# PSUM split by the engine that writes it, and a graph layer's blocks staggered over three blocks' time

## The chip, the cores and the metric

The kernel runs on one core of a Trainium2 chip. The metric is the device time of one execution in microseconds, from the first to the last instruction of the program with what lies directly around it. Three runs of the kernel before gave 17895.24, 17900.07 and 17902.10 us; their median, 17900.07 us, is the time it is measured against. One further execution was recorded by the hardware profiler and took 17875.51 us; every row quoted below comes from that one.

## What is computed

One layer of a graph network on 50,000 nodes of 128 features and 1,650,000 edges, sorted by destination. The reference, cut:

```python
Xs = X[src]
m_data = Xs @ W_data.T + b_data
m_ctrl = Xs @ W_control.T + b_control
msg = jnp.where((edge_types == 0)[:, None], m_data, m_ctrl)
agg = jax.ops.segment_sum(msg, dst, num_segments=X.shape[0])
out = jax.nn.relu(agg + (X @ W_self.T + b_self))
return _layernorm(X + out)
```

The kernel sums rows of X first, for each destination and edge type apart, and multiplies the sums by the weights afterwards.

## The kernel before, in words

The edges are cut into 448 blocks. A block covers at most 124 destination nodes and has two steps of 14 columns of 128 edges, so 28 columns; what is left over of its edges (63 per step with the late ones, "fillers") is put into free places of the columns by arithmetic. All work of a block is spread over four engines.

- **POOL** (GpSimd) does nothing in the loop but fetch rows: one indirect DMA per column (`gathers`, L499) brings 128 rows of X into a slot `y`. Seven columns make a pass and share a slot; a block has four passes (q = 0 to 3), and there are ten slots (`SLOTS`). The first DMA of a pass waits until PE has finished with the slot's pass of ten passes ago; the other six wait for nothing.
- **PE** (TensorE) multiplies each column by its one-hot matrix (`products`, L518: in fp32, which makes two weight loads and two matmuls a column, 28 instructions a pass), adds the counts (L522), spreads the filler list over the partitions (`spread`, L353), counts replaced places (`left_out_columns`, L390), builds the correction for them (`left_out_numbers`, L406 and L409) and computes the finished block (`own_part` and `layer`, L543 to L554).
- **DVE** (VectorE) makes the one-hot matrices two blocks ahead (`onehot` L474, `counts` L482), places the fillers up to five blocks ahead (`fill`, L362 to L383), turns L390's result into a matrix (`left_out_matrix`, L397 and L398), moves the node features (`positions`, L468), adds the products to the running sums (`begin_sums` L538, `add` L527), and does ReLU, moments and normalisation (`moments`, L559 to L567, `store`, L589).
- **ACT** takes one square root per pair of blocks (L580), **SP** issues the plain loads and stores.

Every ten blocks `columns` (L240 to L341) prepares a group of blocks, with a matrix `rank` on PE (L287, L289).

The order on each engine is written out by hand in the main loop of `straight` (from `for b in range(NBLK)`), and each engine runs its instructions strictly in that order. Semaphores are placed from the tiles: an instruction that writes a PSUM tile waits for the earlier readers of that tile's bank. In the kernel before one bank, `small`, holds four things: constants that DVE reads in `onehot` and `fill` (`num_ps`, `rank_no_ps`), a small copy that DVE writes in `fill` (L362), the filler list that PE writes in `spread`, and the column that PE writes in L390 and DVE reads in L397. So PE's L390 stands behind DVE's `oh`, and PE's L353 behind DVE's `at`.

In block b the kernel before adds the last products of block b-1 to the sums first, computes the layer of b-1 on PE after the second pass, and adds the first step of block b as soon as its second pass is done.

Of the kernel before, what the change touches and what calls it, by code (L numbers as in the profile page):

```python
# [11 lines left out]
F32 = mybir.dt.float32  # L12
BF16 = mybir.dt.bfloat16
# [19 lines left out]
R = 14  # L33
# [59 lines left out]
def straight(ctx, tc, c, x, x_t, edges_t, edges_f, dst_first, first_p, out):  # L93
# [22 lines left out]
    ps_r = ctx.enter_context(tc.tile_pool(name="ps_r", bufs=1, space=bass.MemoryType.PSUM))  # L116
# [12 lines left out]
    FILL = Q * FX + C1  # L129
# [36 lines left out]
    nc.vector.tensor_scalar(row_of[:, 1, :], c["ident"][:GB, :GB], float(COLS), None, op0=ALU.mult)  # L166

    loads = {}
    col_g, rk_g, stay_g, cb_g, vp_g, late_g = {}, {}, {}, {}, {}, {}
    stats = keep.tile([P, 2, 2, GROUPS], F32, name="stats")  # L170
    nc.vector.memset(stats, 0.0)
# [83 lines left out]
    def packed(src, col):  # L255
# [5 lines left out]
        nc.vector.scalar_tensor_tensor(v, src, float(COLS), lim, op0=ALU.mult, op1=ALU.add)  # L261
        return v

    def columns(g):

        a = loads.pop(g)
# [7 lines left out]
        def first_of_f(rel, d):  # L274
# [3 lines left out]

        h = eds.tile([P, GB, Q, H], BF16, name="h_loop", bufs=1)
        nc.vector.memset(h, 0.0)
        nc.vector.tensor_tensor(h[:, :, :, :R], a["s"].rearrange(steps, r=R1)[:, :, :, :R],
                                a["d"].rearrange(steps, r=R1)[:, :, :, :R], op=ALU.is_equal)
        rank = ps_r.tile([P, GB * Q, H], F32, name="rank")
        hs_ = h.rearrange("p b q r -> p (b q) r")
        nc.tensor.matmul(rank, below, hs_, start=True, stop=False)  # L287
        for r in range(R):
            nc.tensor.matmul(rank[:, :, r + 1:], ones_b, hs_[:, :, r:r + 1].to_broadcast([P, GB * Q, R - r]),  # L289
                             start=False, stop=r == R - 1)  # L290
# [55 lines left out]
    def spread(b):  # L346

        if plain(b):
            return
        g, i = divmod(b, GB)  # L350
        vf = lists[b % 2][:, :Q * FX]
        for m in range(3):
            nc.tensor.matmul(vf, row_of[:, min(m, 1), i:i + 1].to_broadcast([GB, P]), vp_g[g][:, m, :], start=m == 0, stop=m == 2)  # L353

    def fill(b):

        if plain(b):
            return
        g, i = divmod(b, GB)
        two = lists[b % 2]  # L360
        vf, cb = two[:, :Q * FX], two[:, Q * FX:]
# [9 lines left out]
        nc.vector.tensor_reduce(v, new, AX.X, ALU.add)  # L371
        vi = fil.tile([P, C1], I32, name="vi")
        nc.vector.tensor_tensor(vi, v, stay_g[g][:, i, :], op=ALU.add)
        idx = fil.tile([P, C1], I32, name="idx", bufs=RAHEAD + 2)
        nc.vector.tensor_single_scalar(idx, vi, COLS.bit_length() - 1, op=ALU.logical_shift_right)
        nc.vector.scalar_tensor_tensor(col_g[g][:, i, :], idx, -float(COLS), vi, op0=ALU.mult, op1=ALU.add)
        idxs[b] = idx

        old = fil.tile([P, C1, FX], F32, name="old", bufs=1)
        nc.vector.tensor_tensor(old, m, cb[:, :, None].to_broadcast([P, C1, FX]), op=ALU.mult)  # L380
        by = fil.tile([P, Q, FX], BF16, name="by")
        with nc.allow_low_precision(reason="whole numbers below 256, one of them not 0"):
            nc.vector.tensor_reduce(by, old.rearrange("p (q r) f -> p q f r", r=R1), AX.X, ALU.add)  # L383
        bys[b] = by
# [60 lines left out]
    def window(b):  # L445
        if b % SPAN:
            return
        n = min(SPAN, NBLK - b)
        w = b // SPAN
        _, regs = nc.values_load_multi_w_load_instructions(  # L450
            base_i[0:1, w, :1 + n], engines=[SP], min_val=0, max_val=(N - B) * ROW,
            skip_runtime_bounds_check_because=CLAMPED)
        for i in range(n):
            bases[b + i] = regs[1 + i]
        at = nc.s_assert_within(regs[0], 0, (N - WIDE) * 4, skip_runtime_bounds_check_because=CLAMPED)
        xw = stp.tile([P, WIDE], F32, name="xw")
        nc.sync.dma_start(xw.bitcast(U8), x_t_bytes[:, bass.ds(at, 4 * WIDE)])
        wides[w] = xw

# [114 lines left out]
    def pair(b):  # L574

        return together(b) if b == together(b)[-1] else ()
# [19 lines left out]
    def find_bad():  # L596
# [29 lines left out]
        nc.vector.tensor_reduce(total, gap, AX.X, ALU.add)  # L626
        nc.vector.tensor_copy(c["bad"], total)

    columns(0)
    spread(1)  # L630
    fill(1)
# [1 line left out]
    window(0)  # L633
    onehot(0)
    counts(0)
    left_out_columns(1)
    left_out_matrix(1)
    positions(0)
    clear_sums()
    spread(2)  # L640
    fill(2)
    for b in range(1, AHEAD):
        onehot(b)
        counts(b)
    made, fresh = 2, [2]
    ready = []
    for b in range(NBLK):
        if b == NBLK - 2:
            find_bad()
        if b == NBLK - 1:  # L650
            if pair(b - 2):
                store(pair(b - 2))
                ready.extend(pair(b - 2))
            while ready:
                store_rows(ready.pop(0))
        if b + 3 < NBLK:
            window(b + 3)
        g, i = divmod(b, GB)
# [4 lines left out]
        for f in fresh:  # L663
            spread(f)
        if b > 0:
            add(b - 1, steps_of(b - 1)[-1])
        begin_sums(b)
        if b == NBLK - 1:
            layer(b - 1)
            moments(b - 1)  # L670
            root(pair(b - 1))
            own_part(b)
            store(pair(b - 1))
            for done in pair(b - 1):
                store_rows(done)
            for step, ks in passes_of(b):
                if ks:
                    products(b, step, ks)
                    if step not in steps_of(b)[-1:] and ks[-1] == chunks_of(b, step)[-1]:
                        add(b, step)  # L680
            break
        if b + AHEAD < NBLK:
            onehot(b + AHEAD)
            counts(b + AHEAD)
        last = steps_of(b)[-1:]
        for q, (step, ks) in enumerate(passes_of(b)):
            if ks:
                products(b, step, ks)
            if q == 0:
                for f in due:  # L690
                    left_out_columns(f)
                for f in fresh:
                    fill(f)
            if q == 1 and b > 0:
                layer(b - 1)
            if q == 1:
                left_out_numbers(b + 1)
            if ks and step not in last and ks[-1] == chunks_of(b, step)[-1]:
                add(b, step)
            if q == 1 and b > 0:  # L700
                moments(b - 1)
            if q == 1:
                for f in due:
                    left_out_matrix(f)
            if q == 1 and b + 1 < NBLK:
                positions(b + 1)
                left_out_rows(b + 1)
            if q == 2 and i == GB // 2 - 1 and g + 1 < GROUPS:
                columns(g + 1)
            if q == 1 and b > 1 and pair(b - 2):  # L710
                store(pair(b - 2))
                ready.extend(pair(b - 2))
            if q == 3 and b > 0 and pair(b - 1):
                root(pair(b - 1))
            if q == 3 and ready:
                store_rows(ready.pop(0))
    b = NBLK - 1
    add(b, steps_of(b)[-1])
    layer(b)
    moments(b)  # L720
    root(pair(b))
# [332 lines left out]
```

## Time and profile before

| | |
|---|---|
| median of three runs | 17900.07 us |
| the profiled execution | 17875.51 us |
| its span, first to last instruction | 17873.8 us |
| share of the span busy: PE / weight loads / DVE / POOL | 39% / 34% / 66% / 66% |
| mean granted TensorE clock | 0.598 |
| indirect DMAs on POOL | 12,516 and 6 for the last block |
| mean time per block (28 columns) | 17873.8 / 447.1 = 39.98 us |

No engine is busy for more than two thirds of the span, and the busy shares are the same in all forty slices of it, so that one block looks much like any other. A row of the timeline gives the start, the duration, the engine, the line and operation, and, in brackets, how long the engine had been idle before and what ended that; "issue" is idle time for which the profile shows no semaphore, "remote" a semaphore whose sender it could not tell. PEld is the weight load, which shares PE's instruction stream. In the table of windows, (x) after a busy time is the number of instructions in that stretch.

### The profile page before, as it was taken

To read this page: it belongs to the slowest core of one execution; us is meant where nothing else is said; L and a number is where in the kernel's file an instruction comes from. 1 tells how busy PE (TensorE), PEld (TensorE's weight loads), DVE (VectorE), ACT (ScalarE), POOL (GpSimd) and SP (SyncE) were. 2 spreads that over 40 slices of the span, in tenths; PEclk is the share of its full clock that TensorE was granted. 3 is DMA by queue.
4 is the path that set the end of the run, shared out by engine and by line. 5 is a ranking of instruction groups with operands and counts; after the bars stand their busy time and mean duration, and the time that the engine had idled before them with its cause. 6 is when DMAs were issued, how large, how long until landed. Compare 5 with 4: busy or idle time off the path is not lost.

```text
span 17873.8 us, 103324 instructions
## 1 busy us (share of the span) xinstructions
PE 6946.3 (39%) x34670; PEld 6006.5 (34%) x34671; DVE 11876.6 (66%) x12324; ACT 69.8 (0%) x231; POOL 11880.6 (66%) x12532
## 2 busy tenths in 40 slices
PE   3433434333343333333333333343333333333334
PEld 2333333333333333333333333333333333333333
DVE  7666666666666666666666666666666666666665
ACT  0000000000000000000000000000000000000000
POOL 6666666666666666666666666666666666666666
PEclk6656555555565555666555555565555555555556
DMA  2211112112121111212212112121121211212111
GB/s 53 52 50 50 51 50 52 50 50 52 50 51 50 50 51 50 52 50 52 51 50 52 50 50 52 50 52 50 50 51 50 52 50 50 52 50 51 50 50 47
DMA packets 474808, 905.71 MB, mean 51 GB/s; under 512 B 204473, under 2 KB 260872, under 8 KB 474270
## 3 DMA queue, kind: packets, MB, share of 16 engines
q0 software_dynamic: 400736, 821.40, 18.1%
q1 hardware_dynamic: 73096, 77.42, 1.5%
q8 instruction: 279, 4.57, 0.1%
q14 instruction: 259, 2.12, 0.0%
q10 hardware_dynamic: 438, 0.20, 0.0%
HBM read 869.76 MB, written 28.44 MB: 50 GB/s over the span
## 4 chain that ended last, share of the span: by engine, by line
DVE 51%; another core or an unknown queue 27%; issue 17%; PE 5%; DVEq 0%; DMA 0%; ACT 0%; ACTq 0%
DVE cnt L482 14%; DVE oh L474 9%; DVE m L364 4%; DVE v_new L371 4%; DVE new L367 4%; DVE old L380 4%; PE acc L518 4%; DVE sums L527 2%; DVE sums L538 1%; DVE z L398 1%; DVE st L562 1%; DVE h L560 1%; DVE xT L468 1%; DVE h L559 0%
## 5 line engine op out<-in xcount | busy, mean ns | idle before, releaser
L499 POOL DMA_INDIRECT y<-in_x,idx x12516 | 11873.2, 949 | 5958.3 <-issue 3574.2
L518 PE MATMUL acc<-oh,y 128*128 128x128 f32 x25044 | 5433.2, 373 | 4761.1 <-issue 4725.3
L518 PEld LDWEIGHTS acc<-oh,y 128*128 128x128 f32 x25044 | 4793.6, 277 | 7175.2 <-issue 5937.1
L527 DVE TENSOR_TENSOR sums<-acc,sums 128x192 f32 x895 | 314.8, 352 | 4137.2 <-remote 4003.0
L482 DVE TENSOR_REDUCE cnt<-oh 128x256 bf16<-128x3584 f32 x448 | 2807.1, 6266 | 15.4
L474 DVE TENSOR_TENSOR oh<-col,small 128x3584 f32<-128x3584 f32 x448 | 1737.4, 3878 | 255.4 <-remote 185.4
L383 DVE TENSOR_REDUCE by<-old 128x126 bf16<-128x1764 f32 x446 | 1466.5, 3288 | 15.5
L353 PE MATMUL small<-v_f,row_of 10*128 10x126 bf16 x1338 | 231.4, 287 | 2709.3 <-DVE st L562 1642.5
L353 PEld LDWEIGHTS <-row_of 10*128 10x128 bf16 x1338 | 127.1, 112 | 2895.1 <-issue 2882.5
L364 DVE TENSOR_TENSOR m<-rk,small 128x1764 f32<-128x1764 f32 x446 | 888.5, 1992 | 17.7 <-remote 1.7
L367 DVE TENSOR_TENSOR new<-m,small 128x1764 f32<-128x1764 f32 x446 | 888.1, 1991 | 15.2
L371 DVE TENSOR_REDUCE v_new<-new 128x28 f32<-128x1764 f32 x446 | 887.9, 1991 | 15.2
L380 DVE TENSOR_TENSOR old<-m,small 128x1764 f32<-128x1764 f32 x446 | 884.8, 1984 | 0.0
L390 PE MATMUL small<-ones_b,by 128*126 128x1 bf16 x446 | 72.6, 163 | 1917.8 <-DVE oh L474 1352.2
L522 PE MATMUL acc<-cnt,to_row 128*128 128x64 bf16 x1790 | 293.2, 224 | 669.7 <-issue 665.9
L554 PE MATMUL po<-wmsgT,sums 128*124 128x128 f32 x1792 | 428.5, 367 | 82.5 <-issue 79.7
L522 PEld LDWEIGHTS <-to_row 128*128 128x128 bf16 x1790 | 225.7, 126 | 678.6 <-issue 646.4
L559 DVE COPY h<-po 124x128 f32<-124x128 f32 x448 | 125.8, 281 | 439.0 <-PE acc L518 306.2
L554 PEld LDWEIGHTS po<-wmsgT,sums 128*124 128x124 f32 x1792 | 314.0, 241 | 196.8 <-issue 169.7
L415 DVE TENSOR_TENSOR pl<-pl,xT 128x248 f32<-128x248 f32 x446 | 189.4, 425 | 208.1 <-remote 136.3
L552 PE MATMUL po<-bias,sums 3*124 3x128 f32 x896 | 281.7, 396 | 91.4 <-issue 90.9
L289 PEld LDWEIGHTS <-ones_b 128*128 128x128 bf16 x630 | 82.0, 150 | 639.7 <-issue 620.2
(142 smaller groups left out, 3673.6 us busy)
## 6 DMA issues: line engine op xcount, KB each, us to landing
y<-in_x,idx POOLq DMA_INDIRECT x12516
xw<-in_x_t SPq DMA_DIRECT2D x56, 496.0 KB
out<-o SPq DMA_DIRECT2D x448, 62.0 KB
sdt<-in_edges_t SPq DMA_DIRECT2D x45, 420.0 KB
sdt_f<-in_edges_f SPq DMA_DIRECT2D x45, 14.8 KB
first_i<-in_dst_first SPq DMA_DIRECT2D x1, 450.0 KB
y<-in_x,sdt POOLq DMA_INDIRECT x6
w_all<-in_L_gnn_W_data ACTq DMA_DIRECT2D x1, 64.0 KB
```

What stands on the lines that cost most here:

```text
L364: nc.vector.tensor_tensor(m, rk_g[g][:, i, :, None].to_broadcast([P, C1, FX]), rank_no_ps[:, None, :].to_broadcast([P, C1, FX]), op=ALU.is ...
L367: nc.vector.tensor_tensor(new.rearrange("p (q r) f -> p q r f", r=R1), m.rearrange("p (q r) f -> p q r f", r=R1), vf.rearrange("p (q f) -> ...
L371: nc.vector.tensor_reduce(v, new, AX.X, ALU.add)
L380: nc.vector.tensor_tensor(old, m, cb[:, :, None].to_broadcast([P, C1, FX]), op=ALU.mult)
L383: nc.vector.tensor_reduce(by, old.rearrange("p (q r) f -> p q f r", r=R1), AX.X, ALU.add)
L474: nc.vector.tensor_tensor(oh, col_g[g][:, i, :, None].to_broadcast([P, C1, 2 * W]), num_ps[:, None, :].to_broadcast([P, C1, 2 * W]), op=AL ...
L482: nc.vector.tensor_reduce(cnt, ohs[b].rearrange("p (q r) w -> p q w r", r=R1), AX.X, ALU.add)
L499: copy = nc.gpsimd.indirect_dma_start(out=y[:r, k % PASS, :].bitcast(U8), out_offset=None, in_=x_rows, in_offset=bass.IndirectOffsetOnAxis ...
L518: nc.tensor.matmul(acc[:, :2, :].rearrange("p t w -> p (t w)"), y[:r, k % PASS, :], ohs[b][:r, column(k), :], start=k == of_step[0], stop= ...
L522: nc.tensor.matmul(acc[:, 2, :], to_row[:, t, :], cnts[b][:, q, t * W:(t + 1) * W], start=t == 0, stop=t == 1)
L527: nc.vector.tensor_tensor(part, accs.pop((b, q)), part, op=ALU.add)
L554: nc.tensor.matmul(po, a[:, t, :B], c["wmsgT"][:, t * D:(t + 1) * D], start=False, stop=t == 1)
```

## The change

Three things are changed together; no instruction of arithmetic is added or removed.

First, the PSUM bank `small` becomes two: `fixed`, which only DVE writes (the constants and the copy of L362, two of them by turns), and `made`, which only PE writes (one filler list in place of two, the matrix `rank`, which had a bank of its own, and the column of `left_out_columns`).

Second, the work of a block is spread over more blocks. DVE adds both steps of block b-1 in block b, after its fills, in one go with `begin_sums`; PE computes the layer of block b-2 in block b; the correction of b-1 is multiplied out in block b (before, that of b+1). `left_out_matrix` runs one block after its `left_out_columns`. `onehot` and `counts` come first in DVE's block, then `fill`.

Third, buffers follow: one more one-hot matrix (`ohp`), four `by`, two wide feature tiles in place of three. The first half of `columns` becomes `loops` and `ranks`, one block earlier.

```diff
-    ohp = ctx.enter_context(tc.tile_pool(name="ohp", bufs=AHEAD + 1))
+    ohp = ctx.enter_context(tc.tile_pool(name="ohp", bufs=AHEAD + 2))
...
-    small = keep_ps.tile([P, 2 * W + FX + 2 * FILL + 2], F32, name="small")
-    num_ps, rank_no_ps = small[:, :2 * W], small[:, 2 * W:2 * W + FX]
-    lists = [small[:, 2 * W + FX + i * FILL:][:, :FILL] for i in range(2)]
-    sums_at = [small[:Q * FX, 2 * W + FX + 2 * FILL + i:][:, :1] for i in range(2)]
+    fixed = keep_ps.tile([P, 2 * W + FX + 2 * C1], F32, name="fixed")
+    num_ps, rank_no_ps = fixed[:, :2 * W], fixed[:, 2 * W:2 * W + FX]
+    olds = [fixed[:, 2 * W + FX + i * C1:][:, :C1] for i in range(2)]
+    made_ps = keep_ps.tile([P, Q * FX + GS * (R + 1) + 2], F32, name="made")
...
-        by = fil.tile([P, Q, FX], BF16, name="by")
+        by = fil.tile([P, Q, FX], BF16, name="by", bufs=4)
...
-        xw = stp.tile([P, WIDE], F32, name="xw")
+        xw = stp.tile([P, WIDE], F32, name="xw", bufs=2)
...
-        if b > 0:
-            add(b - 1, steps_of(b - 1)[-1])
-        begin_sums(b)
...
+        for f in fresh:
+            spread(f)
+            fill(f)
         for q, (step, ks) in enumerate(passes_of(b)):
             if ks:
                 products(b, step, ks)
-            if q == 0:
...
-            if q == 1 and b > 0:
-                layer(b - 1)
-            if q == 1:
-                left_out_numbers(b + 1)
-            if ks and step not in last and ks[-1] == chunks_of(b, step)[-1]:
-                add(b, step)
...
+            if q == 1 and b > 0:
+                if b > 1:
+                    layer(b - 2)
+                left_out_numbers(b - 1)
+            if q == 2:
+                for f in late_pcs:
+                    left_out_matrix(f)
                 for f in due:
                     left_out_columns(f)
...
+            if q == 2 and b > 0:
+                positions(b - 1)
+                left_out_rows(b - 1)
+                begin_sums(b - 1)
+                for step in steps_of(b - 1):
+                    add(b - 1, step)
+                if b > 1:
+                    moments(b - 2)
```

How the instructions stand, first on PE around the filler list and the column of replaced places; `small` and `made` are the PSUM banks, `acc` the products' bank, and the names in brackets are what the instruction waits for (`landed` the rows' arrival). Before, from the end of one block into the next:

```order
L353 MATMUL small<-v_f,row_of 128x126 [waits DVE_49]
L518 MATMUL acc<-oh,y 128x128 [waits landed0,PE_sequencer_49]
...
L390 LDWEIGHTS by
L390 MATMUL small<-ones_b,by 126x1 [waits DVE_49]
L518 MATMUL acc<-oh,y 128x128 [waits landed1,PE_sequencer_49]
...
L554 MATMUL po<-wmsgT,sums_187 124x128 x2
```

The change, the same stretch:

```order
L361 MATMUL made<-v_f,row_of 128x126
L525 MATMUL acc<-oh,y 128x128 [waits landed2,PE_sequencer_49,DVE_49]
...
L525 MATMUL acc<-oh,y 128x128 [waits landed3,PE_sequencer_49]
...
L561 MATMUL po<-wmsgT,sums_185 124x128 x2
...
L525 MATMUL acc<-oh,y 128x128 [waits landed4,PE_sequencer_49]
...
L397 LDWEIGHTS by
L397 MATMUL made<-ones_b,by 126x1 [waits DVE_49]
L525 MATMUL acc<-oh,y 128x128 [waits landed5,PE_sequencer_49]
```

The column's matmul has moved from behind the first pass to behind the third, and waits there for DVE's copy `at` of the same block (L404) instead of its `oh`. The list's matmul waits for DVE no more, since that wait already stood ahead of it. The first product of a block, which did not wait for DVE, now has a third wait, for the sums that free its bank `acc`; the third wait takes an instruction of its own on PE, 398 more in the whole program, and DVE has 445 more of that kind.

On DVE, from the sums into the next block; `acc` are the products, `pl` the correction, `po` the layer's output. Before:

```order
L527 TENSOR_TENSOR sums_188<-acc,sums_188 128x3x64 [waits PE_49]
...
L538 TENSOR_TENSOR sums_189<-pl,sums_188 128x3x124 [waits DVE_49]
L474 TENSOR_TENSOR oh<-col,small 128x3584 [waits PE_49]
L482 TENSOR_REDUCE cnt<-oh 128x256 [waits DVE_49]
L362 COPY small<-cb 128x28 [waits PE_49]
...
L527 TENSOR_TENSOR sums_189<-acc,sums_189 128x3x64 [waits PE_49]
L559 COPY h<-po 124x128 [waits PE_49]
...
L415 TENSOR_TENSOR pl<-pl,xT 128x2x124 [waits DVE_49,PE_49]
```

The change:

```order
L422 TENSOR_TENSOR pl<-pl,xT 128x2x124 [waits DVE_49,PE_49]
...
L545 TENSOR_TENSOR sums_186<-pl,sums_185 128x3x124 [waits DVE_49]
...
L534 TENSOR_TENSOR sums_186<-acc,sums_186 128x3x64 [waits DVE_49]
...
L534 TENSOR_TENSOR sums_186<-acc,sums_186 128x3x64 [waits DVE_49]
L566 COPY h<-po 124x128
...
L481 TENSOR_TENSOR oh<-col,fixed 128x3584
L489 TENSOR_REDUCE cnt<-oh 128x256 [waits DVE_49]
L369 COPY fixed<-cb 128x28
...
L374 TENSOR_TENSOR new<-m,made 128x1764 [waits DVE_49,PE_49]
```

Of six places in a block at which DVE waits for PE two are left: the correction (L422) and the filler list (L374). The order of POOL's instructions and what they wait for is as before.

More of the change, by code (lines that the diff above doesn't have):

```diff
@@ L168, in straight @@
     loads = {}
+    hs_g = {}
     col_g, rk_g, stay_g, cb_g, vp_g, late_g = {}, {}, {}, {}, {}, {}
@@ L262, in packed, with loops, ranks @@
         return v
+    def loops(g):
+        a = loads[g]
+        steps = "p b (q r) -> p b q r"
+        h = eds.tile([P, GB, Q, H], BF16, name="h_loop", bufs=1)
+        nc.vector.memset(h, 0.0)
+        nc.vector.tensor_tensor(h[:, :, :, :R], a["s"].rearrange(steps, r=R1)[:, :, :, :R],
+                                a["d"].rearrange(steps, r=R1)[:, :, :, :R], op=ALU.is_equal)
+        hs_g[g] = h.rearrange("p b q r -> p (b q) r")
+    def ranks(g):
+        hs_ = hs_g[g]
+        nc.tensor.matmul(rank, below, hs_, start=True, stop=False)
+        for r in range(R):
+            nc.tensor.matmul(rank[:, :, r + 1:], ones_b, hs_[:, :, r:r + 1].to_broadcast([P, GB * Q, R - r]),
+                             start=False, stop=r == R - 1)
     def columns(g):
@@ L277, in first_of_f @@
                    begin_p.rearrange("b (q g) -> b q g", q=Q)[:, :, g:g + 1].to_broadcast([GB, Q, FX]))
[L281 to L290, printed above, removed]
+        hs_ = hs_g.pop(g)
         col, rel, nz = columns_of(a["d"], a["t"], first_of, "")
@@ L350, in spread @@
         g, i = divmod(b, GB)
-        vf = lists[b % 2][:, :Q * FX]
         for m in range(3):
-            nc.tensor.matmul(vf, row_of[:, min(m, 1), i:i + 1].to_broadcast([GB, P]), vp_g[g][:, m, :], start=m == 0, stop=m == 2)
+            nc.tensor.matmul(vf_ps, row_of[:, min(m, 1), i:i + 1].to_broadcast([GB, P]), vp_g[g][:, m, :], start=m == 0, stop=m == 2)
     def fill(b):
@@ L359, in fill @@
         g, i = divmod(b, GB)
-        two = lists[b % 2]
-        vf, cb = two[:, :Q * FX], two[:, Q * FX:]
+        vf, cb = vf_ps, olds[b % 2]
         nc.vector.tensor_copy(cb, cb_g[g][:, i, :])
@@ L627, in find_bad @@
         nc.vector.tensor_copy(c["bad"], total)
+    loops(0)
+    ranks(0)
     columns(0)
@@ L644, in straight @@
         counts(b)
-    made, fresh = 2, [2]
-    ready = []
-    for b in range(NBLK):
+    made, fresh = 2, [1, 2]
+    late_pcs, ready = [], []
+    for b in range(NBLK - 1):
         if b == NBLK - 2:
             find_bad()
[L650 to L655, printed above, removed]
         if b + 3 < NBLK:
@@ L684, in straight @@
             counts(b + AHEAD)
-        last = steps_of(b)[-1:]
+        if i == GB // 2 - 2 and g + 1 < GROUPS:
+            loops(g + 1)
+        for f in fresh:
+            spread(f)
+            fill(f)
         for q, (step, ks) in enumerate(passes_of(b)):
@@ L688, in straight @@
                 products(b, step, ks)
-            if q == 0:
+            if q == 1 and b > 0:
[5 more added lines that the diff above has]
+                    left_out_matrix(f)
                 for f in due:
                     left_out_columns(f)
-                for f in fresh:
-                    fill(f)
-            if q == 1 and b > 0:
-                layer(b - 1)
-            if q == 1:
-                left_out_numbers(b + 1)
-            if ks and step not in last and ks[-1] == chunks_of(b, step)[-1]:
[L699 to L714, printed above, removed]
+                late_pcs = due
+                if i == GB // 2 - 2 and g + 1 < GROUPS:
+                    ranks(g + 1)
+            if q == 2 and b > 0:
[6 more added lines that the diff above has]
+                    moments(b - 2)
+                if b > 2 and pair(b - 3):
+                    store(pair(b - 3))
+                    ready.extend(pair(b - 3))
+                if b > 1 and pair(b - 2):
+                    root(pair(b - 2))
+                if i == GB // 2 - 1 and g + 1 < GROUPS:
+                    columns(g + 1)
             if q == 3 and ready:
@@ L717, in straight @@
     b = NBLK - 1
-    add(b, steps_of(b)[-1])
+    layer(b - 2)
+    left_out_numbers(b - 1)
+    positions(b - 1)
+    left_out_rows(b - 1)
+    begin_sums(b - 1)
+    for step in steps_of(b - 1):
+        add(b - 1, step)
+    moments(b - 2)
+    if pair(b - 3):
+        store(pair(b - 3))
+        ready.extend(pair(b - 3))
+    if pair(b - 2):
+        root(pair(b - 2))
+    layer(b - 1)
+    if pair(b - 2):
+        store(pair(b - 2))
+        ready.extend(pair(b - 2))
+    while ready:
+        store_rows(ready.pop(0))
+    positions(b)
+    begin_sums(b)
+    moments(b - 1)
+    root(pair(b - 1))
+    own_part(b)
+    store(pair(b - 1))
+    for done in pair(b - 1):
+        store_rows(done)
+    for step, ks in passes_of(b):
+        if ks:
+            products(b, step, ks)
+            if ks[-1] == chunks_of(b, step)[-1]:
+                add(b, step)
     layer(b)
```

21 lines of the change are left out of this document (2 added, 19 removed).

## Prediction

> **What bounds the kernel now.** I read the page's busy sums and chain first, then the costliest groups, then the waits of POOL's fetches, a stretch of the timeline around one stop, and last a table of windows.
>
> ```profile
> span 17873.8 us, 103324 instructions
> PE 6946.3 (39%) x34670; PEld 6006.5 (34%) x34671; DVE 11876.6 (66%) x12324; ACT 69.8 (0%) x231; POOL 11880.6 (66%) x12532
> DVE 51%; another core or an unknown queue 27%; issue 17%; PE 5%; DVEq 0%; DMA 0%; ACT 0%; ACTq 0%
> ```
>
> No engine is full, and the chain puts half of the span on DVE. That reading I don't take: DVE's 11,876.6 us are 26.6 us in each of the 447 blocks of the main loop, and a block takes 17,873.8 / 447.1 = 39.98 us, so the chain runs through DVE only because its work happens to end late. What has no slack is POOL:
>
> ```profile
> L499 POOL DMA_INDIRECT y<-in_x,idx x12516: 939/947/1582, 3.3 to 17832.7; - x199
> its engine sat idle before it (us, times) until:
>   issue: 3575.7, 11728
>   remote: 1937.7, 403
>   PE acc L522: 200.2, 102
>   PE small L353: 96.9, 20
> ```
>
> A fetch lasts 0.947 us, and between two lie 3575.7 / 11,728 = 0.305 us for which nothing is shown: one fetch every 1.252 us, whatever the rest does. 12,516 of them are 15,670 us. From the first to the last pass 17,829 us, so that some 2,160 us are stops. Nearly all of it is waits of 1,937.7 / 403 = 4.8 us, about one a block: 28 x 1.252 = 35.05 us of fetches and one stop of 4.83 us above the usual gap give 39.9 us, which is the block. So the question is what makes POOL stop once a block.
>
> ```profile
> 9013.04 0.95 POOL L499 DMA_INDIRECT y<-in_x,idx  x1 [0.30 <-issue]
> 9013.93 0.29 PEld L518 LDWEIGHTS acc<-oh,y 128*128 128x128 f32 x1 [2.51 <-issue]
> 9014.64 0.37 PE L518 MATMUL acc<-oh,y 128*128 128x128 f32 x1 [1.73 <-issue]
> 9016.03 0.29 PEld L518 LDWEIGHTS acc<-oh,y 128*128 128x128 f32 x1 [1.81 <-issue]
> 9018.83 1.65 PE L518 MATMUL acc<-oh,y 128*128 128x128 f32 x7 [0.33 <-issue]
> 9019.07 0.36 DVE L527 TENSOR_TENSOR sums<-acc,sums 128x192 f32 x1 [13.27 <-remote]
> 9019.12 0.95 POOL L499 DMA_INDIRECT y<-in_x,idx  x1 [5.13 <-remote]
> 9019.92 3.88 DVE L474 TENSOR_TENSOR oh<-col,small 128x3584 f32<-128x3584 f32 x1
> 9023.85 0.16 PE L390 MATMUL small<-ones_b,by 128*126 128x1 bf16 x1 [3.37 <-DVE oh L474]
> ```
>
> This is one stop. Up to 9018.8 PE creeps: each load or matmul takes 0.7 us or more beyond itself, with no wait named ("issue"). POOL issues its last fetch of the stretch at 9013.04, then stands 5.13 us. At 9018.83, 4.8 us after that fetch ended, everything lets go at once: PE runs seven matmuls on end, DVE gets an answer that it had stood 13.27 us for, POOL starts again. The same picture returns once a block. How much PE gets done between two such stops the windows show (columns: PE, PEld, DVE, ACT, POOL busy with their instructions, clock, DMA share, GB/s):
>
> ```profile
> 9218.40:9231.80 13.40, 10.02 (x63) 9.39 (x64) 13.05 (x6) 0.00 (x0) 10.05 (x11) 0.67 0.20 49
> 9231.80:9258.30 26.50, 4.05 (x15) 2.40 (x14) 12.77 (x20) 0.00 (x0) 16.44 (x18) 0.55 0.25 67
> 9417.80:9448.60 30.80, 15.23 (x72) 13.64 (x73) 29.13 (x34) 0.29 (x1) 23.15 (x25) 0.56 0.20 50
> 9448.60:9457.70 9.10, 1.52 (x7) 1.32 (x6) 1.88 (x8) 0.00 (x0) 4.07 (x4) 0.69 0.14 36
> 9016.00:9018.80 2.80, 0.74 (x2) 0.86 (x3) 0.00 (x0) 0.00 (x0) 0.00 (x0) 0.50 0.00 0
> 9018.80:9021.20 2.40, 1.65 (x7) 1.46 (x7) 2.10 (x3) 0.00 (x0) 1.78 (x2) 0.50 0.11 27
> ```
>
> Two blocks, each a fast stretch and a creep. In the first PE ran 63 + 64 = 127 instructions at 9.5 a us, then 29 in 26.5 us, 1.1 a us. In the second, where it was held by waits in between, 145 in 30.8 us, then 13 in 9.1 us. So the fast stretch ends neither after a time nor after a fixed count: 18 instructions more go with 17.4 us more, about one a us, the pace of the creep. I read it as a store that a stop fills: 127 - 13.4 x 1.03 = **113 instructions**, and one a us trickles in. DVE ran 6 instructions in the one stretch and 34 in the other, which shows no charge for them. In the emptiest part of the stop, 9016.0 to 9018.8, the DMA engines moved nothing. What the store is I can't see; that its price is 4.83 / 113 = 0.043 us of POOL's time per PE instruction is an estimate from these rows. A block needs (34,670 + 34,671 + 1,791) / 447 = 159 with PE's separate waits,
>
> ```profile
> L506 PEldq EVENT_SEMAPHORE  x1791: 51/51/51, 75.5 to 17862.1; - x199
> ```
>
> and gets 113 + 39.9 x 1.03 = 154 from one stop: one stop a block, and now and then one more.
>
> **The change part by part.** *The order of the work.* The waits between PE and DVE that it removes look large:
>
> ```profile
> PE small L390 <- DVE oh L474: 1352.2, 352, 13.9
> PE small L353 <- DVE st L562: 1642.5, 211, 11.5
> L527 DVE TENSOR_TENSOR sums<-acc,sums 128x192 f32 x895 | 314.8, 352 | 4137.2 <-remote 4003.0
> ```
>
> Those are 7,000 us in all. I cost them at nothing, since they fill time that the stop sets: PE's 156 instructions would take 16 us of 39.9 at the fast pace, DVE's work 26.6. POOL's own wait, for PE to be done with its slot's pass of ten passes ago, stays. If that cover were gone (POOL never stopping), a block would still be 35.05 us, above both.
>
> *PE's new waits*, on the first product of a block, are 398 instructions. At the price above 398 x 0.043 = **+17 us**. Below, they cost nothing, as DVE's seem to; above, DVE's 445 would count too, +19 more. I take the PE ones, because PE's are what the windows tie to the stop.
>
> *Where PE stands in the fast stretch.* In the row of 9018.80 PE did 7 + 7 instructions in 2.4 us, and then stood 3.37 us for `oh`, with one load ahead. At 9.5 a us it could have done 23, so nine more. If what runs straight after the stop is not yet charged (the fetches have just begun again: two in that window), the stop would carry nine more, 122 in place of 113, and the time saved is 9 x 0.043 x 447 = 172 us; if it is charged like all else, nothing. PE stood there in 352 of 446 blocks, 0.79. In the changed kernel L390's place (now L397, behind the third pass) waits for `at`, but the piece after the first pass is free. I take half, for want of a row that decides: 172 x 0.79 x 0.5 = **-68 us**, with 0 and -172 kept. A loss isn't excluded either: the new wait of the first product, or L397's, may be what PE meets there; that is a rival below.
>
> *The two halves of the PSUM bank* take from `fill` and `onehot` DVE's waits on PE. Behind them on DVE stood 26.6 us of work in a block of 39.9, so nothing, as above. The filler list, now single, makes DVE's L374 wait for L361 of its own block; behind it is the rest of the fill (`new`, `v_new`, `old` at 2.0 us and `by` at 3.3, rows of the groups below), and for it waits PE's L397. This fits into the block as long as each goes once per stop.
>
> ```profile
> L383 DVE TENSOR_REDUCE by<-old 128x126 bf16<-128x1764 f32 x446 | 1466.5, 3288 | 15.5
> L371 DVE TENSOR_REDUCE v_new<-new 128x28 f32<-128x1764 f32 x446 | 887.9, 1991 | 15.2
> ```
>
> *The end.* After the last fetch came 41.1 us. One more block's addition and layer is now left for there; its length before:
>
> ```profile
> 17863.93 0.36 DVE L527 TENSOR_TENSOR sums<-acc,sums 128x192 f32 x1 [0.82 <-PE acc L522]
> 17867.27 0.35 DVE L589 TENSOR_SCALAR o<-h,mv,rstd 124x128 f32<-124x128 f32 x1
> ```
>
> 3.7 us from addition to result, so **+4 us**. Buffers and `loops`/`ranks` move no count of instructions: nothing.
>
> **Sum**: 17,875.5 + 17 - 68 + 4 = 17,828.5 us for an execution under the profiler. The median of the runs lies 17,900.07 - 17,875.51 = 24.6 us above it, so 17,853 us, 47 us or 0.26% less than before. About 0.2%, 36 us, is what a measurement of this kernel can tell from no change.
>
> **Rivals.** *The change doesn't touch what stops POOL.* Then 17,900 + 21 = 17,921 us. For it: POOL's waits and slots are as before, and the stop lasts 4.8 us after the last fetch wherever PE and DVE stood. This is also what the Trainium skill, Perfetto Trace Analysis, section Optimization Strategy, has of repeated equal gaps: they can mean that there aren't enough buffers for the next tile. That row agrees in that POOL stands at the first fetch of a slot, and the ten slots stay ten.
>
> *POOL never stops.* If the stops came from PE and DVE holding each other, and PE now kept within ten passes: 15,670 + 3.3 + 41.1 + 4 + 24.6 = 15,743 us. The same section's rule, to find the gaps of the most contended engine and let what it waits for start sooner, is what the change does by it. For it: 102 of POOL's waits end with L522, and DVE stood 4,003 us for PE. Against it: PE creeps with no DVE wait named.
>
> *All of the early time counts*: 17,921 - 172 = 17,749 us.
>
> *PE stands right after the stop more than before.* The addition that frees `acc` comes on DVE behind the correction (L422), which needs PE's answer; if that answer too is seen only when the creep ends, PE meets the first product's new wait, or L397's, exactly in the 2.4 us in which it ran 14 instructions. At half their charge, as above, 14 x 0.043 x 447 x 0.5 = 134 us lost: 17,921 + 134 = 18,055 us. It decides when PE's first passage after the stop is a new block's first product in most blocks. Beyond it, each tenth of the blocks that needs a second stop costs 45 x 4.83 = 216 us.
>
> **How the numbers follow.** Forecast 0.52, no touch 0.14, all early time 0.08, never stops 0.10, stands more 0.16. Forecast's own range is 17,770 to 17,960 (0 to the full gain, and DVE's waits charged): faster 0.26, same 0.15, slower 0.11. No touch: 0.02, 0.08, 0.04. All early time and never stops are faster, 0.18; stands more is slower, 0.16. Together faster 0.46, same 0.23, slower 0.31. The range goes to 17,600 below, leaving out the never-stopping 0.10, and to 18,200 above, which takes in the fifth rival with half a tenth of second stops and leaves out its worse half, 0.08.
>
> **What would show it.** Right: POOL's row keeps its 1.25 us and 450 to 475 waits of 5 us; DVE's 4,003 us `remote` at the additions shrink and turn up at L422 and L374; PE still creeps at one a us. The gain shows as fewer stops (about 15) and a fast stretch with more than 113 above the trickle. Wrong: stops gone or halved with PE still at 159 a block (then the store is no count of instructions), or stops longer than 5.1 us (then PE itself is too late for its slot), or a block above 41 us with DVE standing at L374 for a list that PE has not reached.

## The result and the profile after: no change that the measurement can tell

The changed kernel took 17,907.57 us (median of 12 runs, 17,905.47 to 17,916.31), the kernel before 17,895.57 us in 12 runs beside it: a ratio of 1.0007, 95% interval 0.9998 to 1.0016. The forecast was 17,853 us, 0.26% faster, with a range from 17,600 to 18,200; the rival "the change doesn't touch what stops POOL" had 17,921.

From the page of the changed kernel, the span, the busy sums, and the groups that answer to those of before (busy, mean ns of one, then the idle time ahead and what ended most of it):

```profile
span 17910.8 us, 104168 instructions
PE 7106.6 (40%) x34670; PEld 6022.9 (34%) x34671; DVE 11867.3 (66%) x12324; ACT 70.0 (0%) x231; POOL 11881.7 (66%) x12532
L506 POOL DMA_INDIRECT y<-in_x,idx x12516 | 11874.4, 949 | 5978.4 <-issue 3621.8
L374 DVE TENSOR_TENSOR new<-m,made 128x1764 f32<-128x1764 f32 x446 | 888.6, 1992 | 3428.5 <-remote 3114.9
L422 DVE TENSOR_TENSOR pl<-pl,xT 128x248 f32<-128x248 f32 x446 | 189.5, 425 | 1892.6 <-remote 1120.7
L397 PE MATMUL made<-ones_b,by 128*126 128x1 bf16 x446 | 76.2, 172 | 1712.6 <-issue 1004.5
L534 DVE TENSOR_TENSOR sums<-acc,sums 128x192 f32 x895 | 319.8, 357 | 33.3 <-PE acc L529 2.5
```

DVE's 4,137 us ahead of the additions have shrunk to 33 us, and 3,428 + 1,893 us now stand ahead of the filler list and the correction. The waits moved as the edit says, and the time did not follow. POOL's waits, from the view of its fetch line:

```profile
L506 POOL DMA_INDIRECT y<-in_x,idx x12516: 942/947/1522, 3.3 to 17853.9; - x199
  issue: 3623.0, 11878
  remote: 2053.9, 467
  PE acc L525: 133.3, 42
  PEq L513: 131.5, 60
```

The stops are there as before: 2,054 us in 467 waits behind an unnamed sender (1,938 in 403 before), and POOL's whole idle time ahead of its fetches is 5,978 us in place of 5,958. The last fetch of the loop starts at 17,853.9 instead of 17,832.7 us, 21.2 us later, and from there to the end of the span pass 56.9 us instead of 41.1. That is the 37 us between the two profiled spans. The medians of the runs differ by 12 only: the profiled execution of the kernel before (17,875.51 us) lies 20 us below the median of its kernel, that of the change (17,912.93 us) 5 us above, so that 25 of the 37 us lie between executions and not between kernels.

### The profile page after: what moved, and what is told of

It reads as the page before. It is cut to its first block, busy times and chain, and to the rows that moved or that the text cites. A ratio compares the mean times of both kernels' runs of the same rounds, so it can differ in the third digit from the quotient of the medians.

```text
span 17910.8 us, 104168 instructions
## 1 busy us (share of the span) xinstructions
PE 7106.6 (40%) x34670; PEld 6022.9 (34%) x34671; DVE 11867.3 (66%) x12324; ACT 70.0 (0%) x231; POOL 11881.7 (66%) x12532
## 4 chain that ended last, share of the span: by engine, by line
DVE 48%; another core or an unknown queue 21%; issue 21%; PE 10%; DVEq 0%; DMA 0%; ACTq 0%; ACT 0%
DVE cnt L489 10%; DVE oh L481 7%; PE acc L525 7%; DVE by L390 6%; DVE new L374 4%; DVE v_new L378 4%; DVE m L371 4%; DVE old L387 4%; DVE sums L534 1%; PE po L561 1%; DVE o L596 1%; DVE sums L545 1%; DVE z L405 1%; DVE h L567 1%
## 5 line engine op out<-in xcount | busy, mean ns | idle before, releaser
L525 PE MATMUL acc<-oh,y 128*128 128x128 f32 x25044 | 5583.2, 369 | 5981.5 <-issue 5916.1
L374 DVE TENSOR_TENSOR new<-m,made 128x1764 f32<-128x1764 f32 x446 | 888.6, 1992 | 3428.5 <-remote 3114.9
L481 DVE TENSOR_TENSOR oh<-col,fixed 128x3584 f32<-128x3584 f32 x448 | 1732.8, 3868 | 0.0
L422 DVE TENSOR_TENSOR pl<-pl,xT 128x248 f32<-128x248 f32 x446 | 189.5, 425 | 1892.6 <-remote 1120.7
L371 DVE TENSOR_TENSOR m<-rk,fixed 128x1764 f32<-128x1764 f32 x446 | 888.4, 1992 | 17.8 <-remote 1.7
L387 DVE TENSOR_TENSOR old<-m,fixed 128x1764 f32<-128x1764 f32 x446 | 884.9, 1984 | 0.0
L361 PE MATMUL made<-v_f,row_of 10*128 10x126 bf16 x1338 | 233.4, 265 | 1505.8 <-issue 920.9
L397 PE MATMUL made<-ones_b,by 128*126 128x1 bf16 x446 | 76.2, 172 | 1712.6 <-issue 1004.5
L551 PE MATMUL po<-wselfT,xT 128*124 128x128 f32 x896 | 251.2, 354 | 297.6 <-issue 297.4
L551 PEld LDWEIGHTS po<-wselfT,xT 128*124 128x124 f32 x896 | 213.3, 277 | 320.8 <-issue 320.8
```

What stands on the lines that cost most here:

```text
L481: nc.vector.tensor_tensor(oh, col_g[g][:, i, :, None].to_broadcast([P, C1, 2 * W]), num_ps[:, None, :].to_broadcast([P, C1, 2 * W]), op=AL ...
L525: nc.tensor.matmul(acc[:, :2, :].rearrange("p t w -> p (t w)"), y[:r, k % PASS, :], ohs[b][:r, column(k), :], start=k == of_step[0], stop= ...
```

## The experiments

**Two kinds of session.** The runs of one session share a chip and stand beside the kernel before on it. That kernel took 15,706.88, 15,686.30 and 15,684.90 us in the first three sessions and 17,902.64 us in the fourth. The records name chip 13, chip 2, chip 1 and chip 2 again, so that one chip gave both values. Within a session the runs of one kernel agree to 0.2%. I call the two kinds sessions without stops and sessions with stops; the result above comes from one with stops. Times are compared within a session only, unless it is said.

### First session (the kernel before: 15,706.88 us, no stops)

More PE instructions, in the changed kernel:

```diff
...
             accs[b, q] = ps.tile([P, 3, W], F32, name="acc")
+            for _ in range(6):
+                nc.tensor.matmul(accs[b, q][:, 2, 0:1], ones_b, ones_b[:, 0:1], start=True, stop=True)
```

> The changed kernel (17,908 us) with 12 small bf16 matmuls a block more, 24 instructions with their weight loads, about 2.5 us of PE's time in a block in which it is idle for more than 20. Theory (a store of PE instructions that only a stop of POOL's fetches fills): 24 x 447 x 0.043 = +461 us, so about 18,370 (18,250 to 18,480), with some 95 stops more. Rival A (the waits between PE and DVE set the block): PE has the time to spare, so 17,890 to 17,960. Rival B (the ten slots and the landing of the rows set the stop): 17,908 within 20.

Measured 15,719.63 us, 1.0009 of before (0.9999 to 1.0018). More DVE instructions, in the changed kernel:

```diff
+    spare = keep.tile([P, 1], F32, name="spare")
...
+        for _ in range(24):
+            nc.vector.memset(spare, 0.0)
```

> The changed kernel with 24 tiny VectorE writes of one column a block more, some 1.5 us of DVE's time. Theory (only PE's instructions are charged): 17,908 within 36. If the store holds the instructions of every engine: +461 us as for PE. Rival A (PE and DVE in a chain): up to 1.5 us x 447 = +670 us. Rival B: 17,908.

Measured 15,715.96 us, 1.0005 (0.9995 to 1.0015). Half the product instructions, in the changed kernel:

```diff
-            nc.tensor.matmul(acc[:, :2, :].rearrange("p t w -> p (t w)"), y[:r, k % PASS, :], ohs[b][:r, column(k), :],
+            nc.tensor.matmul(acc[:, :2, :].rearrange("p t w -> p (t w)"), y[:r, k % PASS, :].bitcast(BF16)[:, 1::2], ohs[b][:r, column(k), :].bitcast(BF16)[:, 1::2],
```

> The changed kernel with each column multiplied by the upper 16 bits of its fetched numbers as bf16 (the lower 16 are left out), so that a column takes one weight load and one matmul in place of two and two: 25,044 PE instructions less; fetches, bytes, DVE and all waits as before. Theory: n stops with 113 n + 1.03 T = 71,530 - 25,044 and T = 15,714 + 4.83 n give n = 257 and T = 16,960 us (16,800 to 17,150). Rival A and Rival B: PE had time to spare in any case, so 17,908 within 40.

Measured 15,718.73 us, 1.0007 (0.9998 to 1.0017). The split of the bank alone, in the kernel before:

```diff
-    small = keep_ps.tile([P, 2 * W + FX + 2 * FILL + 2], F32, name="small")
...
+    fixed = keep_ps.tile([P, 2 * W + FX + 2 * C1], F32, name="fixed")
...
+    made_ps = ps_r.tile([P, Q * FX + GS * (R + 1) + 2], F32, name="made")
...
-        for f in fresh:
+        for f in fresh[:1]:
             spread(f)
...
+                    if f != fresh[0]:
+                        spread(f)
                     fill(f)
```

> The kernel before with the PSUM bank divided by the engine that writes it and nothing staggered (a second filler list of a block is spread after the first was used). Theory: PE's count is the same, so 17,896 within 36, though the waits of PE for oh at L390 (352 in the trace before) go. Rival A: the 1,352 us that PE stood there, or a part of it, are saved: 16,900 to 17,700.

Measured 15,709.70 us, 1.0002 (0.9992 to 1.0011).

None of these four could tell the theories apart, because what they were to act on was absent. From the page of the kernel with more PE instructions, and then from the one with half the product instructions:

```profile
PE 7447.9 (47%) x40040; PEld 6767.1 (43%) x40041; DVE 11875.5 (76%) x12324; ACT 69.8 (0%) x231; POOL 11852.7 (76%) x12532
L506 POOL DMA_INDIRECT y<-in_x,idx x12516 | 11845.4, 946 | 3815.1 <-issue 3809.1
```

```profile
PE 3379.9 (22%) x22148; PEld 2669.3 (17%) x22149; DVE 11874.6 (76%) x12324; ACT 69.8 (0%) x231; POOL 11880.6 (76%) x12532
L525 PE MATMUL acc<-oh,y 128*128 128x128 bf16 x12522 | 1660.8, 305 | 12023.7 <-PEq L513 11932.5
```

POOL's idle time is 3,815 us, all of it the 0.3 us between two fetches; the 2,160 us of stops are gone, in all four kernels alike. PE stands in its own queue (L513, the wait for landed rows). POOL fetches without a break, and neither 40,040 nor 22,148 matmuls matter. What does follow: the stops are not a necessary result of this program on a Trainium2 chip.

### Second session (the kernel before: 15,686.30 us, no stops)

```diff
-SLOTS = 10
+SLOTS = 6
```

> The changed kernel with six slots of seven fetched columns in place of ten. On a chip where the kernel before takes about 15,707 us (POOL never stops, PE takes each pass 1.7 us after its last fetch): six slots are enough, 15,715 within 36. On a chip where it takes about 17,900 us (one stop a block): by the store theory the number of stops hangs on PE's instructions alone, 17,908 within 60; by Rival B (the ten slots set the stop) POOL stops after six passes and more often, at least 447 x 4.83 x (10/6 - 1) = 1,440 us more, 19,300.

Measured 15,706.28 us, 1.0013 (1.0002 to 1.0024): 20 us above the kernel before, and within what was expected without stops. Of the stops it tells nothing, so whether the number of slots matters with stops was not tried. Fewer fetches, in the changed kernel:

```diff
+FETCH = 2
...
-        for k in ks:
+        fetched = ks[:FETCH] if b < NBLK - 1 else ks
+        for k in fetched:
...
-        seen[i] += 16 * len(ks)
+        seen[i] += 16 * len(fetched)
...
-            nc.tensor.matmul(..., y[:r, k % PASS, :], ...
+            at = k % PASS if b == NBLK - 1 else k % PASS % FETCH
+            nc.tensor.matmul(..., y[:r, at, :], ...
```

> The changed kernel with two of seven columns of a pass fetched, the other products made from those two (the rest of the rows is left out): POOL has 8 fetches a block, 10 us in place of 35. PE's and DVE's instructions are the same. On either kind of chip: if the fetches alone bind, the next bound is DVE's 26.6 us a block plus its waits for PE, 12,000 to 13,500 us. If on a chip with stops PE creeps because of POOL's fetches, the creep goes with them and the time is the same there as on the other; if PE creeps for a reason of its own, it stays above 15,000 there.

Measured 12,329.96 us, within the expected 12,000 to 13,500. DVE is the bound behind the fetches, as the page's busy row shows:

```profile
span 12328.3 us, 95228 instructions
PE 5052.4 (41%) x34670; PEld 4669.1 (38%) x34671; DVE 11862.7 (96%) x12324; ACT 69.8 (1%) x231; POOL 3383.1 (27%) x3592
```

### Third session (the kernel before: 15,684.90 us, no stops)

Two edits of the first session once more, and the changed kernel itself.

> The bf16 products again (the lower 16 bits of the fetched numbers left out, 25,044 PE instructions fewer), for a chip on which the kernel before takes about 17,900 us and POOL stops once a block. There, by the store theory: 257 stops, 16,960 us (16,800 to 17,150); if the stops don't hang on the count of PE's instructions: 17,908 within 40. On a chip without stops: 15,700 to 15,720, as the kernel before there, which tells nothing of the store.

Measured 15,688.51 us, 1.0003 (0.9993 to 1.0013).

> The 24 more PE instructions a block again. On a chip with stops, by the store theory: 18,370 us (18,250 to 18,480) and some 95 stops more; if PE's count doesn't matter: 17,890 to 17,960. On a chip without stops: 15,700 to 15,725.

Measured 15,690.92 us, 1.0004 (0.9994 to 1.0014). Both are inconclusive for the store, like the first time.

> The changed kernel as it is, beside the kernel before on one chip. With stops: 17,908 against 17,896. Without stops nothing of PE's or DVE's order is on the path but the end behind the last fetch: +4 us (the predicted term for one more addition and layer there), within 15 of the kernel before.

Measured 15,691.50 us against 15,684.90, 1.0004 (0.9995 to 1.0013). Its span, its view of POOL's fetch line and its product group:

```profile
span 15689.2 us, 104168 instructions
...
L506 POOL DMA_INDIRECT y<-in_x,idx x12516: 940/944/1819, 3.3 to 15661.6; - x199
  issue: 3810.2, 12503
...
L525 PE MATMUL acc<-oh,y 128*128 128x128 f32 x25044 | 5924.8, 429 | 8122.6 <-PEq L513 7739.1
```

15,661.6 - 3.3 us for 12,515 steps from fetch to fetch are 1.251 us each, the same pace as between the stops of the first trace. That is all of the time but the 28 us behind the last fetch; the 6.6 us more than the kernel before are no difference that the interval tells from none.

### Fourth session (the kernel before: 17,902.64 us, with stops)

The edit with two of seven columns fetched, in the kernel before:

> The kernel before with two of seven columns of a pass fetched and the other products made from those two (the rest of the rows left out), to be set beside the changed kernel with the same edit, 12,330 us, where DVE was busy for 96% of the span. Theory that the waits between PE and DVE cost nothing in either kernel, being covered by DVE's own 26.6 us a block: 12,330 within 150. Rival: the waits that the change removes (about 7,000 us in the trace before, of which L390's on oh and L353's on st need no fetch) show as soon as the fetches don't cover them: 13,000 to 15,000.

Measured 12,203.41 us. The same with the bank split and nothing staggered:

> The same with two of seven columns fetched (the rest left out), in the kernel before with the PSUM bank divided and nothing staggered. If the split alone removes what shows there, it is at 12,330 like the changed kernel; if the stagger does, it is where the kernel before with two columns is; by the first theory all three are within 150 us.

Measured 12,226.14 us. From the pages of the two, in that order:

```profile
span 12200.6 us, 94384 instructions
PE 6011.1 (49%) x34670; PEld 5522.5 (45%) x34671; DVE 11797.5 (97%) x12324; ACT 69.8 (1%) x231; POOL 3397.5 (28%) x3592
L521 PE MATMUL acc<-oh,y 128*128 128x128 f32 x25044 | 4635.6, 362 | 4.1 <-issue 4.1
L354 PE MATMUL small<-v_f,row_of 10*128 10x126 bf16 x1338 | 212.7, 285 | 4124.6 <-DVE at L398 4093.1
L530 DVE TENSOR_TENSOR sums<-acc,sums 128x192 f32 x895 | 311.3, 348 | 6.0 <-PE acc L525 5.8
```

```profile
span 12224.4 us, 94832 instructions
PE 4995.5 (41%) x34670; PEld 4735.7 (39%) x34671; DVE 11792.6 (96%) x12324; ACT 69.8 (1%) x231; POOL 3393.4 (28%) x3592
```

Two things are to be seen. The three kernels lie within 127 us of each other, as the first theory has it (the changed kernel's 12,330 us are from a session without stops, so that this is only a rough comparison). PE's waits for DVE, which the change removes, cost nothing in the kernel before even where the fetches no longer cover them: PE still stands 4,125 us ahead of the filler list, and DVE is busy for 97% of the span, 96% with the bank split. DVE's waits for PE ahead of the additions, 4,137 us in the trace of before, are down to 6 us by themselves, so this run doesn't test those. And PE's creep is gone with the fetches, in a session with stops: ahead of the products PE stood 4.1 us with no wait named, where it was 4,725 us in the trace of before, with the same 34,670 matmuls in a shorter time.

Six of seven columns fetched, in the changed kernel (FETCH = 6):

> The changed kernel with six of seven columns fetched (one column's rows left out): 24 fetches a block in place of 28. If POOL's pace of 1.252 us a fetch is all that sets the time on a chip without stops: 15,691 - 4 x 447 x 1.252 = 13,453 us within 30. If something else comes up first (DVE with its waits for PE): above 13,500.

Measured 15,427.42 us; the expectation holds for a session without stops, and this one had them. The run tells two readings of the stops apart. By the prediction's store, 113 n + 1.03 T = 71,530 instructions with n stops, and T = 13,479 + 4.83 n (10,728 fetches at 1.252 us, 3 us ahead and 45 us behind), so n = 489 and T = 15,841 us. By a fixed time per fetch, 17,908 - 1,788 x 1.426 = 15,358 us, where 1.426 is the changed kernel's (17,853.9 - 3.3) / 12,515. The measurement lies 414 us from the one and 69 us from the other. These 69 us are more than the runs scatter: a fetch cost (15,376.8 - 3.2) / 10,727 = 1.433 us here, 0.5% more than in the changed kernel, and why is not shown. The view of POOL's fetch line in this run:

```profile
L508 POOL DMA_INDIRECT y<-in_x,idx x10728: 938/944/1575, 3.2 to 15376.8; - x199
```

The same is seen inside the traces. The table of windows, each from the first fetch after one stop to the first after a later one (POOL's count is the fetches between; PE and PEld are PE's instructions). The windows of 18 to 28 fetches hold no other stop; those of 56, 70 and 72 run over two to four shorter ones. The kernel before:

```profile
8240.76:8270.87 30.11, 12.19 (x63) 10.86 (x62) 21.89 (x45) 0.29 (x1) 19.86 (x21) 0.61 0.18 46
8001.67:8041.53 39.86, 14.86 (x78) 13.86 (x78) 25.20 (x23) 0.29 (x1) 26.47 (x28) 0.67 0.18 46
8689.95:8769.79 79.84, 32.42 (x154) 27.44 (x154) 51.56 (x48) 0.29 (x1) 53.00 (x56) 0.61 0.19 48
```

The changed kernel:

```profile
8211.85:8241.97 30.12, 14.72 (x78) 12.65 (x78) 16.89 (x17) 0.30 (x1) 19.86 (x21) 0.61 0.16 47
9868.82:9969.12 100.30, 40.45 (x201) 34.37 (x201) 85.99 (x109) 0.29 (x1) 66.52 (x70) 0.60 0.19 54
```

The changed kernel with six columns fetched:

```profile
11538.74:11564.60 25.86, 12.31 (x73) 10.72 (x72) 24.89 (x22) 0.30 (x1) 17.04 (x18) 0.70 0.19 47
8032.85:8067.15 34.30, 16.53 (x78) 14.56 (x78) 25.04 (x23) 0.30 (x1) 22.72 (x24) 0.60 0.18 46
10782.56:10885.69 103.13, 49.35 (x231) 42.13 (x231) 76.58 (x72) 0.59 (x2) 68.21 (x72) 0.58 0.19 47
```

From stop to stop 21 fetches took 30.11 us with 125 PE instructions and 30.12 us with 156. Divided by the fetches, the eight windows give 1.434, 1.424, 1.426, 1.434, 1.433, 1.437, 1.429 and 1.432 us. So in the traces with stops a fetch costs about 1.43 us, whatever PE and DVE do meanwhile. The eight windows are no lucky choice. In the trace of before, all 414 stretches of 28 fetches between two stops of more than 2 us took 39.88 us, with a standard deviation of 0.14, while PE ran between 134 and 175 instructions in them.

I read it so: POOL issues a fetch every 1.252 us, runs ahead of the slower average until it meets a wait, and there pays back what it ran ahead, 28 x (1.424 - 1.252) = 4.8 us, 21 x 0.182 = 3.8 us, 24 x 0.177 = 4.2 us. These products are the stops' lengths by the same sums and no second proof. The first fetch after the stop of each of these windows, in the timelines of the kernel before (21 and 28 fetches) and of the one with six columns (24); the idle time holds the usual 0.3 us:

```profile
8270.89 0.95 POOL L499 DMA_INDIRECT y<-in_x,idx  x1 [4.15 <-remote]
8041.55 0.95 POOL L499 DMA_INDIRECT y<-in_x,idx  x1 [5.16 <-remote]
```

```profile
8067.17 0.94 POOL L508 DMA_INDIRECT y<-in_x,idx  x1 [4.56 <-remote]
```

## Why the prediction was right in its range and wrong in its reason

The time lay in the range, but the gain of 47 us did not come, and the range was met by luck: the terms of the sum were small, and any account by which the change costs or saves little ends near 17,900 us.

- **No engine is full, POOL has no slack, and the stops set the block**: right, in sessions with stops. 28 x 1.424 us is the block of 39.9.
- **The removed waits between PE and DVE cost nothing**: right. They moved by thousands of microseconds at an unchanged time, and with two columns fetched the kernel that still has PE's waits for DVE is bound by DVE's own work.
- **"I read it as a store that a stop fills: 127 - 13.4 x 1.03 = 113 instructions"**: this step failed. Two windows carried it, both of 28 fetches, and in them the count of PE's fast instructions did go with the length of the fast stretch. But what was to be explained was the time from stop to stop, and that hangs on the fetches. For the 30.1 us of 21 fetches the store would give 113 + 30.1 x 1.03 = 144 PE instructions; the window in the trace of before has 125, the one in the changed kernel 156. The price of 0.043 us per PE instruction has no basis: a line through the 414 stretches of 28 fetches gives 0.004 us, one through the changed kernel's 379 such stretches -0.005, and one through the 373 stretches of 24 fetches with six columns 0.001. PE's creep goes when the fetches go; whether it comes from the same limit is not shown.
- **+17 us for 398 waits, -68 us for PE's place after the stop**: both followed from that price, and both have to go. The sign that was to show the gain, some 15 stops fewer, did not come either: 467 waits with an unnamed sender in place of 403. The last fetch of the loop came 21 us later in the profiled run, 0.0017 us a fetch. That is no more than the 25 us by which the two profiled executions stand apart from the medians of their kernels, so I put it down to nothing.
- **+4 us at the end**: right without stops, too small with them. Without stops the changed kernel of the third session takes 15,689.2 - 15,661.6 = 27.6 us from the loop's last fetch to the end; the kernel with only the bank split, whose blocks are not staggered, takes 15,709.6 - 15,685.7 = 23.9, which is 3.7 us less:

```profile
span 15709.6 us, 103772 instructions
L497 POOL DMA_INDIRECT y<-in_x,idx x12516: 941/947/1467, 3.3 to 15685.7; - x199
```

With stops the profiled run shows 16 us more than before, of which 4.4 are a stop ahead of the last six fetches:

```profile
17859.20 0.42 DVE L422 TENSOR_TENSOR pl<-pl,xT 128x248 f32<-128x248 f32 x1 [52.05 <-remote]
17859.58 0.95 POOL L506 DMA_INDIRECT y<-in_x,sdt  x1 [4.69 <-remote]
```

In the kernel before these six fetches followed at once (17,834.0 us, 1.3 after the loop's last). DVE had stood 52 us for the correction, and several blocks' additions and layers were still to be done behind it, where the sum counted one. The 12 us between the medians are of this size, but the measurement does not tell them from nothing, and that the end makes all of it was not tried by itself.

- **The rivals**: "the change doesn't touch what stops POOL" was the right one, though its 17,921 us hold the same 17. Its ground, the wait for one of ten slots, is where the stop is paid, not why it is owed. The Trainium skill, Perfetto Trace Analysis, section Optimization Strategy, says that repeated equal gaps can mean too few buffers. The trace of before doesn't bear that out: PE's last product out of the slot that POOL waits for had ended 21 us before POOL began to stand (the median of 461 stops of more than 2 us; at least 5 us in each). "POOL never stops" gave 15,743 us, and that time was met within 0.4%, in the kernel before and after alike: it is what a session without stops gives, and no merit of the change. "All of the early time counts" and "PE stands right after the stop more than before" rest on the same price; the measurement lies some 150 us from their 17,749 and 18,055 us.

Left open: what in a session with stops makes a fetch cost 1.43 us, why the same program, once on the same chip, has sessions without, and why PE creeps and its answers are seen late meanwhile. The rows themselves are not late: a fetch's last DMA packet was through 1.26 us after the fetch ended, as the median, in the trace of before and in that of the changed kernel without stops alike. Yet PE began a pass 66 us after the start of the pass's last fetch in the one, and 2.7 us in the other, as the medians. Whether PE's instruction count has a small share in the 1.43 us was to be told by the kernels with more and with fewer PE instructions, but all four of their runs fell in sessions without stops. The three lines above leave it little room: some 0.005 us per instruction, an eighth of the price in the sum, and with either sign. If the 0.007 us by which a fetch was dearer with six columns came from the 0.92 PE instructions more beside each fetch alone, it would be 0.007 us, a sixth.

## What to carry to other kernels

Before a stall is put down to the engine that looks odd beside it, divide the time from stall to stall by the count of each kind of work in it, over windows in which these counts differ; the one whose quotient stays the same is the first to suspect as the bound, and here one table of windows would have shown it. An engine that runs ahead at a fast pace and stands at regular intervals may be held to a slower average, as POOL was here, and then shortening what others do in that time moves waits but not the end. Run the kernel before anew beside every experiment: it can itself come out 12% apart from one session to another.

## What was not expected of the hardware

The same program took 17,903 us in one session and 15,686 us in another on chip 2, with the same duration of a fetch (a median of 0.944 us with six slots in the one and with six columns in the other) and the same 0.305 us between two. With stops, PE ran 9.5 instructions a microsecond in one part of a stretch and 1.1 in the other, while POOL went on fetching at its full pace in both (11 fetches in the first 13.4 us of the window at 9,218 us); with two of seven columns fetched nothing of the creep was left ahead of the products (4.1 us in place of 4,725). And without stops PE took each product row as it landed, and 25,044 PE instructions fewer or 10,740 more (5,370 matmuls with their loads) were not to be seen in the time.
